# Where a two-layer graph network fetches its last results, turns its raw features and checks its adjacency

## The chip, the cores and the metric

The kernel runs on one core of one Trainium2 chip. TensorE (PE) multiplies matrices, with its weight loads shown as PEld; VectorE is DVE, ScalarE is ACT, GpSimd is POOL and SyncE is SP. SP and POOL also issue most of the DMA transfers, each in the order of its own queue. The metric is the time of one execution on the device in microseconds (us); the median of three executions is compared.

## The reference, cut to what matters

Sixteen graphs of 1024 nodes with 128 features go through two layers. Each normalizes its input, runs four rounds over the graph's 1024 x 1024 adjacency of zeros and ones, and adds the result to its input.

```python
# layer 0: a gated network, per graph
h = relu(layernorm(x))
for i in range(4):
    hw = einsum('bnc,cd->bnd', h, weight[i])
    m = einsum('bjn,bjd->bnd', adj, hw)
    h = gru_cell(m, h, w_ih[i], w_hh[i], b_ih[i], b_hh[i])
x = x + h * mask[:, :, None]
# layer 1: four convolutions; mean and variance go over all graphs and nodes
h = relu(layernorm(x))
for i in range(4):
    h = relu(einsum('bnm,bmc->bnc', adj, h @ W[i]) + b[i])
    mu, var = mean(h, (0, 1)), mean(square(h - mu), (0, 1))
    h = gamma[i] * (h - mu) * rsqrt(var + EPS) + beta[i]
x = x + h
```

## The kernel before, in words

**The gated stage.** Two streams run side by side: `sa` takes the even graphs and `sb` the odd ones, one layer apart by half a step. `half_step(one, two)` does the gates of `two` (`products`, twelve pairs of matmuls in two halves of 512 nodes, then sigmoid, tanh and the DVE arithmetic that ends in `mixed`) and the aggregation of `one` over the adjacency (`agg_step`, L523). `clock[0]` counts the half steps, from 3. In this stage every engine gets its instructions in the order of the program text (`tc.manual_schedule`). Extra work is put into an agenda by `at(n, place, go)` and taken out by `due(place)` at named places of half step n: "beside0" and "beside1" lie after the reset gate of each half, "looks" just after "beside0" and ahead of the first tanh, "gap" after the second half is done and ahead of the aggregation, "start" at the beginning. An instruction in the agenda thus stands in each engine's order at that place, whatever the other engines have reached.

`row_sums` (L602) lets ACT sum rows of the first graph's adjacency; its scratch tile `junk` has the same single buffer as the transposed weights `w_both`, which a matmul (`join_layer`, L488) reads. The sums leave as `degree`, which the convolutions use. `glance` and `look` collect in `low` whether any adjacency value is inexact in bfloat16. After the gated stage the maximum of `low` becomes `worst` (a DVE reduction and a minimum), a one-column matmul adds it over the partitions (`pt_flag`, L1337), and DVE copies it to `flag_i` (L1338), which chooses another path at the very end. These instructions stand outside the hand-written order, so a scheduler places them.

At the end of a graph's four rounds `half_away` transposes the last h in 32 x 32 blocks on DVE and stores it, half by half, to a DRAM tile `pair`, from which it is read back in another order (`pair_in`, L620). For the last two graphs, 14 and 15, the store goes through POOL, and the tail of the layer is done as `chores` during the first convolution: fetch of the pair into the tile `feat[b]`, masked sums and statistics (`masked_sum` L729, `norm_sums` L662 and L663), `factors` (root, reciprocal, and the store of the new x to `xmid_d`, L743), `blocks` (normalization and relu on ACT, L678, written over x), and the store of the result to `ymid_d` (L746).

**The first convolution.** A loop goes over batches b, one graph each. `load_adjT` lets SP load eight row tiles (256 KB each) of the transposed adjacency in bfloat16: even batches into the single tile `block`, odd ones into the ring `half` of eight buffers (`packed`). DVE and ACT cast them to `wide` (a ring of twelve). `first_split` loads y of the next batch through POOL (L1426), after a one-column POOL copy that waits until the tile's earlier reader is done (L1425); ACT rounds it to `hw[0]` (L1429), DVE writes the remainder to `hw[1]` (L1430). `aggregate` does 32 matmuls per batch in two halves. Between the halves PE does `first_weights` of the batch before: ACT copies two banks to `cm` (L1439), PE multiplies (L1440), ACT applies relu into `feat` (L1408) and DVE takes statistics (L1417). In this stage a scheduler fixes each engine's order ahead of time from the program and its own estimates; it may place chores earlier than the text has them, but each engine then runs strictly in that order.

`raw_turned(1)` transposes feat of graph 0 on DVE (L1449), stores it and loads it back through POOL (L1452, L1456), for `raw_split(1)` at the last batch.

Of the kernel before, what the change touches and what calls it, by code (L numbers as in the profile page):

```python
# [8 lines left out]
F32 = mybir.dt.float32  # L9
F32R = mybir.dt.float32r  # L10
BF16 = mybir.dt.bfloat16
# [3 lines left out]
ALU = mybir.AluOpType  # L15
AX = mybir.AxisListType
P = 128
HALF = 512
# [323 lines left out]
def exact_path(  # L342
# [21 lines left out]
    nc = tc.nc  # L364
# [17 lines left out]
    def tmp(name):  # L382
        return ps_t.tile([P, HALF], F32, tag="tmp", name=name)
# [148 lines left out]
    with ExitStack() as st:  # L532
# [83 lines left out]
        def pair_in(d, t, eng=nc.sync):  # L616

            src = d.rearrange("h (t r) (s x) -> s r (h t) x", t=4, s=4)
            for s in range(4):
                eng.dma_start(t[s * 32 : (s + 1) * 32, :].rearrange("r (a x) -> r a x", a=8), src[s])  # L620
# [96 lines left out]
        def half_out(t, src, hf, name, d=None, eng=nc.sync):  # L717
            turned = nc.vector.transpose(by_nodes(t), four_ways(src[:, hf * HALF : (hf + 1) * HALF]))
            return exchange_out(t, f"{name}_{hf}", d, eng), turned

        def cross_tile(name):
            return half_tile(name).bitcast(F32)
# [22 lines left out]
        def store_ymid(b, y):  # L745
            nc.gpsimd.dma_start(ymid_d[b], y)  # L746
# [3 lines left out]
        class Stream:  # L750
# [15 lines left out]
            def sums(self, ks):  # L766
                norm_sums(self.xt, self.norm, ks)
# [93 lines left out]
            def fetch(self):  # L861

                if self.i == 3 and self.b + 2 < B and not written[0]:
                    if self is sa:
                        t = turned_tile(f"stage{self.b + 2}").bitcast(F32)
                        room[0] = [t[:, 2 * q : 2 * q + 2, :].rearrange("p a n -> p (a n)") for q in range(4)]
                    self.stage = room[0]
                    stage_rows(self.b + 2, self.stage, range(2))
# [36 lines left out]
            def half_away(self, hf):  # L905

                if self.i + 1 - hf == L:
                    end = self.b + 2 >= B
                    if hf == 0 and end:
                        self.pair = dram.tile([NH, P, HALF], F32, tag=f"end{self.b}", name=f"pair_end{self.b}")  # L910
                    elif hf == 0:
                        self.pair = rawd.tile([NH, P, HALF], F32, tag="pair", name=f"pair_out{self.b}", bufs=4)
                    eng = nc.gpsimd if end else nc.sync
                    half_out(cross_tile(f"t_out{self.b}_{hf}"), self.new, hf, f"out{self.b}", self.pair[hf], eng)
                elif self.turned_away(self.i + 1 - hf):
                    nm = f"{self.b}_{self.i + 1 - hf}"
                    out, self.last_dve = half_out(cross_tile(f"t_h{nm}_{hf}"), self.new, hf, f"h{nm}")
                    self.outs.append(out)
# [154 lines left out]
        def at(n, place, go):  # L1073
            agenda.setdefault((n, place), []).append(go)
# [9 lines left out]
        def half_step(one, two, gated=None, halfway=None, rest=None):  # L1084

            due("ins")
            due("start")
            if one.i > 0:
                one.halves_back()
            else:  # L1090
                one.hw = hw_tiles(one.b, f"ghw{one.b}_0")
            two.fetch()
            due("load")
            two.products(0)
            two.reset_gate(0)
            due("beside0")
            due("looks")
            two.fetch_more()
            two.candidate(0)
            two.less(0)  # L1100
            two.update_gate(0)
            two.scaled()
            one.high(0)
            one.low(0)
            two.mixed(0)
            two.half_away(0)
            two.first_four()
            if (clock[0], "mid") in agenda or (clock[0], "words") in agenda:
                paced(two.new[:, :1], f"mid{clock[0]}")
                due("words")  # L1110
                due("mid")
            two.products(1)
            two.reset_gate(1)
            one.high(1)
            due("beside1")
            two.first_glances()
            one.low(1)
            two.candidate(1)
            two.less(1)
            two.update_gate(1)  # L1120
            two.last_four()
            two.scaled()
            two.mixed(1)
            two.half_away(1)
            due("outs")
            if gated:
                gated()
            due("gap")
            if (clock[0], "behind") in agenda:
                paced(two.new[:, N - 1 :], f"gap{clock[0]}")  # L1130
                due("behind")
            due("end")
            one.agg_step(0)
            if halfway:
                halfway()
            one.agg_step(1)
            if rest:
                rest()
            two.finish()
            clock[0] += 1  # L1140
# [4 lines left out]
        with tc.manual_schedule(engines=every):  # L1145
# [149 lines left out]
            def ahead(i):  # L1295
                join_layer(i)
                if i == 2:
                    turn_hh(3)
# [1 line left out]
            sa.plan(0)  # L1300
            sb.plan(1)
            for n, place, js in (
                (5, "beside1", (0,)),
                (6, "beside0", (1,)),
                (6, "beside1", (2,)),
                (6, "gap", (3,)),
                (7, "gap", (4, 5, 6)),
                (8, "start", (7,)),
            ):
                at(n, place, lambda js=js: row_sums(sa.rows, js))  # L1310

            def degree_out():
                d = degree_d.rearrange("(s j i o) -> s i o j", s=4, j=4, i=32)
                for k in range(4):
                    nc.gpsimd.dma_start(d[k], by_row[k * 32 : (k + 1) * 32, :].rearrange("i (o j) -> i o j", o=2))

            at(9, "mid", degree_out)
            half_step(sa, sb, looks, lambda: ahead(1))
            half_step(sb, sa, lambda: both(2), lambda: ahead(2), lambda: turn_ih(prep, w_g, 3))
            written[0] = False  # L1320
# [8 lines left out]
                sb.gate_step(hf)  # L1329
                sb.half_away(hf)  # L1330


    worst = small.tile([P, 1], F32, tag="worst", name="worst")
    nc.vector.tensor_reduce(worst, low, axis=AX.X, op=ALU.max)
    nc.vector.tensor_scalar_min(worst, worst, 1.0)
    pt = tmp("pt_flag")
    nc.tensor.matmul(pt[:1, :1], worst, ones, start=True, stop=True)  # L1337
    nc.vector.tensor_copy(flag_i, pt[:1, :1])  # L1338


    feat_pool = ctx.enter_context(tc.tile_pool(name="feat", bufs=1))
# [3 lines left out]
    def load_adjT(b, i):  # L1345
        ts = []
        block = None if b % 2 else turned_tile(f"block{b}_{i}")
        for j in range(NB):
            t = half_tile(f"packed{b}_{i}_{j}") if b % 2 else block[:, j, :]
            nc.sync.dma_start(t, adjT_d[b][j])  # L1350
            r = row_tile(f"wide{b}_{i}_{j}")
            if j % 3 == 1:
                nc.scalar.copy(r, t)  # L1353
            else:
                nc.vector.tensor_copy(r, t)  # L1355
            ts.append(r)
        return ts
# [155 lines left out]
    def chores(s, b):  # L1513

        xt, parts = s.xt, feat[b]
        y = xt.rearrange("p k c -> p (k c)")
        nt = norm_tiles(f"mid{b}")

        def sums(q):
            ks = range(2 * q, 2 * q + 2)  # L1520
            masked_sum(b, xt, parts, ks)
            norm_sums(xt, nt, ks)

        def factors():
            norm_factors(nt)
            store_xmid(b, xt)

        def blocks(hf):
            norm_blocks(xt, y, nt, range(hf * BH, (hf + 1) * BH))

        return [
            (0, lambda: pair_in(s.pair, parts, nc.gpsimd)),
            *((1 + q, lambda q=q: sums(q)) for q in range(4)),
            (4, factors),
            (5, lambda: blocks(0)),
            (6, lambda: blocks(1)),
            (6, lambda: store_ymid(b, y)),
        ]

    late = {}  # L1540
    for s, b, first in ((sa, B - 2, 1), (sb, B - 1, 5)):
        for k, go in chores(s, b):
            late.setdefault(first + k, []).append(go)

# [2 lines left out]
    stats = small.tile([P, B * NH + 1, 6], F32, tag="bn_st", name="stats0")  # L1547
    hw, waiting, hw_last = first_split(0), None, None
    for b in range(B):
        rows = load_adjT(b, 0)  # L1550
        hw_next = first_split(b + 1, hw_last) if b + 1 < B else None
        pm = banks(b, 0)
        aggregate(pm, hw, rows, 0)
        if waiting:
            first_weights(*waiting, stats)
        for go in late.get(b, ()):
            go()
        if b == B - 1:
            hw_next = raw_split(1)
        aggregate(pm, hw, rows, 1)  # L1560
        if b == 4:
            raw_turned(1)
        if b == 2:
            nc.gpsimd.dma_start(degree, degree_d.partition_broadcast(P))
        hw_last, hw, waiting = hw, hw_next, (b, pm)
# [117 lines left out]
```

## Time and profile before

| quantity | value |
|---|---|
| median of three executions | 1773.37 us (1772.59 to 1776.34) |
| the profiled execution | 1774.41 us |
| its span, first to last instruction | 1772.4 us |
| mean granted TensorE clock | 0.996 |
| gated stage | up to 1145.46 us of the span |
| first convolution, batch 0 to batch 6 | 1145.46 to 1210.45 us |
| one half step undisturbed (114.41 to 131.98) | 17.57 us |
| one batch of the first convolution undisturbed | 9.03 us |

The profile shows one execution. For each group of instructions it gives the busy time, the mean time of one, and the idle time of the engine just before, with what ended it. Idle time of PE costs time, since PE is nearly always busy; idle time of another engine costs only where PE waits for it later. A timeline gives start, duration, instruction and, in brackets, the idle time before it and its releaser. All times within the run are microseconds from the span's start.

### The profile page before, as it was taken

How to read it: one execution, taken by the hardware profiler on the slowest of the kernel's cores; microseconds unless marked ns; L12 is line 12 of the kernel's file. 1: busy time of each engine (PE TensorE's matmuls, PEld its weight loads, DVE VectorE, ACT ScalarE, POOL GpSimd, SP SyncE). 2: the span in 40 equal slices, each digit the busy share in tenths (PEclk: the TensorE clock that was granted, in tenths of full speed). 3: DMA queues.
4: the chain of work that ended last, by engine and by line, in shares of the span. 5: the costliest groups of instructions: out<-in, count | busy, mean ns of one | idle time of the engine just before them, and what ended most of it. 6: DMA issues, size and time to landing. Idle time of an engine off the chain costs nothing. (4 is left out here: it accounts for less than half of the span.)

```text
span 1772.4 us, 22193 instructions
## 1 busy us (share of the span) xinstructions
PE 1745.7 (98%) x6654; PEld 1184.6 (67%) x6654; DVE 1321.6 (75%) x2378; ACT 1145.5 (65%) x1821; POOL 398.2 (22%) x452
## 2 busy tenths in 40 slices
PE   9999999999999999999999999998999999999997
PEld 5665656565656565665656555666778888888886
DVE  7777987887787887887888787675666666666665
ACT  6467556656556657565655654467787768768865
POOL 4314323232341331331422423231000001000010
PEclk9999999999999999999999999999999999999999
DMA  8449468368557656746846826899867667757666
GB/s 287 128 117 269 123 178 280 111 172 257 159 161 212 199 154 193 234 132 179 256 126 173 285 87 183 264 306 369 279 217 243 227 248 232 262 201 264 216 232 257
DMA packets 305313, 375.50 MB, mean 212 GB/s; under 512 B 24876, under 2 KB 189520, under 8 KB 305184
## 3 DMA queue, kind: packets, MB, share of 16 engines
q1 hardware_dynamic: 292864, 334.06, 60.5%
q0 software_dynamic: 11792, 39.68, 6.5%
q8 instruction: 54, 0.88, 0.2%
q14 instruction: 75, 0.61, 0.1%
q10 hardware_dynamic: 528, 0.26, 0.0%
HBM read 272.19 MB, written 101.72 MB: 211 GB/s over the span
## 5 line engine op out<-in xcount | busy, mean ns | idle before, releaser
L523 PE MATMUL pm<-row,ghw 128*128 128x512 f32 x2048 | 504.4, 403 | 0.8 <-POOL row L562 0.4
L523 PEld LDWEIGHTS pm<-row,ghw 128*128 128x128 f32 x2048 | 383.8, 188 | 108.1 <-issue 22.5
L523 PE MATMUL pc_m<-wide,chw 128*128 128x512 f32 x1024 | 245.3, 395 | 0.0
L523 PEld LDWEIGHTS pc_m<-wide,chw 128*128 128x128 f32 x1024 | 190.6, 188 | 42.5 <-issue 4.3
L968 ACT COPY m<-pm 128x512 f32<-128x512 f32 x128 | 68.7, 588 | 219.2 <-PE pm L523 219.2
L587 POOL CAST row<-stage 128x1024 fp32r<-128x1024 f32 x112 | 126.8, 1137 | 343.9 <-DMA stage<-in_adj_dram 260.2
L523 PE MATMUL pc_g_r<-wide,chw 128*128 128x512 f32 x464 | 188.3, 406 | 0.4 <-DVE wide L1355 0.4
L523 PE MATMUL pc_g_z<-wide,chw 128*128 128x512 f32 x464 | 181.4, 391 | 0.0
L1030 ACT ACTIVATE r<-r,vecs 128x512 f32<-128x512 f32 x128 | 92.2, 720 | 127.0 <-DVE r L1027 124.9
L633 POOL CAST pair<-row 128x1024 bf16<-128x1024 f32 x128 | 165.8, 1345 | 32.8 <-DVE adjT L639 32.8
L1026 DVE SCALAR_TENSOR_TENSOR r<-g_hn,vecs,r 128x512 f32<-128x512 f32 x128 | 93.2, 728 | 105.0 <-ACT r L1025 54.0
L1355 DVE CAST wide<-packed 128x1024 fp32r<-128x1024 bf16 x160 | 109.3, 690 | 72.8 <-PE pc_g_z L523 50.0
L1355 DVE CAST wide<-block 128x1024 fp32r<-128x1024 bf16 x160 | 109.8, 692 | 67.8 <-PE pc_m L523 40.5
L1353 ACT CAST wide<-packed 128x1024 fp32r<-128x1024 bf16 x96 | 100.9, 1052 | 53.4 <-PE pc_g_z L523 21.1
L1007 PE MATMUL g_r<-m,w_mT 128*128 128x512 f32 x256 | 130.8, 592 | 0.4 <-ACT m L968 0.4
L1007 PE MATMUL g_xn<-m,w_mT 128*128 128x512 f32 x256 | 130.7, 592 | 0.0
L1007 PE MATMUL g_z<-m,w_mT 128*128 128x512 f32 x256 | 130.7, 592 | 0.0
L1353 ACT CAST wide<-block 128x1024 fp32r<-128x1024 bf16 x96 | 100.6, 1049 | 45.0 <-PE pc_g_z L523 20.1
L1025 ACT ACTIVATE r<-g_r,brz 128x512 f32<-128x512 f32 x128 | 87.9, 687 | 57.0 <-PE g_r L1007 56.6
L1417 DVE BATCH_NORM_STATS2 stats<-feat 128x6 f32<-128x512 f32 x129 | 85.3, 683 | 43.0 <-ACT feat L1408 29.8
L1043 DVE TENSOR_TENSOR h<-h,r 128x512 f32<-128x512 f32 x96 | 69.8, 727 | 51.9 <-ACT r L1030 51.5
L1047 DVE TENSOR_TENSOR h<-h,z 128x512 f32<-128x512 f32 x128 | 95.0, 742 | 16.3 <-ACT z L1034 3.6
(200 smaller groups left out, 2908.5 us busy)
## 6 DMA issues: line engine op xcount, KB each, us to landing
block<-adjT_d SPq DMA_DIRECT2D x256, 256.0 KB, 4.7
packed<-adjT_d SPq DMA_DIRECT2D x256, 256.0 KB, 5.5
stage<-in_adj_dram SPq DMA_DIRECT2D x120, 512.0 KB, 5.6
adjT_d<-adjT SPq DMA_DIRECT2D x64, 512.0 KB, 7.3
cross_h<-t_h SPq DMA_DIRECT2D x94, 256.0 KB, 2.1
n_h<-cross_h SPq DMA_DIRECT2D x376, 64.0 KB, 2.1
xmid_d<-x POOLq DMA_DIRECT2D x16, 512.0 KB, 3.8
x<-in_x_dram SPq DMA_DIRECT2D x15, 512.0 KB, 4.4
```

The costliest lines, as they stand in the source:

```text
L523: nc.tensor.matmul(pm[hf], hw[s][:, j * P : (j + 1) * P], rows[j][:, hf * HALF : (hf + 1) * HALF], start=(j == 0 and s == 0), stop=(j == N ...
L587: nc.gpsimd.tensor_copy(t, stage[j % 4])
L633: nc.gpsimd.tensor_copy(halves[:, :, o], rows[4 * o + j].bitcast(F32))
L1007: nc.tensor.matmul(po, wT[:, i, g * C : (g + 1) * C], rhs, start=start, stop=stop)
L1025: nc.scalar.activation(r, pr, AF.Sigmoid, bias=brz[:, 3 * i : 3 * i + 1])
L1026: nc.vector.scalar_tensor_tensor(r, phn, b_hn(i), r, ALU.add, ALU.mult)
L1030: nc.scalar.activation(self.r, self.r, AF.Tanh, bias=b_in(self.i))
L1043: nc.vector.tensor_sub(ho, hin, self.r)
L1047: nc.vector.tensor_mul(ho, ho, self.z)
L1353: nc.scalar.copy(r, t)
L1355: nc.vector.tensor_copy(r, t)
L1417: nc.vector.bn_stats(stats[:, b * NH + hf + k, :], dst)
```

## The change

Five things move; no arithmetic is taken out or added.

- The fetch of the last h (graphs 14 and 15) gets a POOL copy ahead of it that reads the current batch's `hw[1]`, so it waits for that DVE remainder. Chores begin one batch later in the text (2 and 6 instead of 1 and 5), and `blocks` a further batch later.
- The transposed halves of the last h go to a tile of the `pair` ring instead of two tiles of the `half` ring. DVE's casts of batch 1 are ordered behind the last DVE instruction of the gated stage; in the resulting order of SP, the loads of batch 1 stand ahead of those of batch 2.
- `raw_turned(1)` moves from batch 4 to batch 12, the thirteenth.
- The row sum of row 0 moves from "beside1" to "gap" in half step 5, that of row 4 from "gap" to "looks" in half step 7.
- The flag's reduction, minimum and matmul go into the hand-written order, in the gap of half step 60 (B * L - 2 * L + 4), and the copy to `flag_i` into the gap of half step 61. Before, the scheduler had them in half steps 58 and 59.

```diff
+                    if end and hf == 0:
+                        t = work.tile([P, 2 * N], BF16, tag="pair", name=f"t_end{self.b}", bufs=3).bitcast(F32)
+                        self.ends = [t[:, k * HALF : (k + 1) * HALF] for k in range(NH)]
+                    t = self.ends[hf] if end else cross_tile(f"t_out{self.b}_{hf}")
+                    half_out(t, self.new, hf, f"out{self.b}", self.pair[hf], eng)
...
-                (5, "beside1", (0,)),
+                (5, "gap", (0,)),
...
-                (7, "gap", (4, 5, 6)),
+                (7, "looks", (4,)),
+                (7, "gap", (5, 6)),
...
+            def worst_of_all():
+                worst = small.tile([P, 1], F32, tag="worst", name="worst")
+                nc.vector.tensor_reduce(worst, low, axis=AX.X, op=ALU.max)
+                nc.vector.tensor_scalar_min(worst, worst, 1.0)
+                pt = tmp("pt_flag")
+                nc.tensor.matmul(pt[:1, :1], worst, ones, start=True, stop=True)
+                at(end + 5, "gap", lambda: nc.vector.tensor_copy(flag_i, pt[:1, :1]))
+
+            end = B * L - 2 * L
+            at(end + 4, "gap", worst_of_all)
...
+        def fetch(seen):
+            nc.gpsimd.tensor_copy(parts[:, :1], seen[:, :1].bitcast(F32))
+            pair_in(s.pair, parts, nc.gpsimd)
...
-            (5, lambda: blocks(0)),
-            (6, lambda: blocks(1)),
-            (6, lambda: store_ymid(b, y)),
+            (6, lambda seen: blocks(0)),
+            (7, lambda seen: blocks(1)),
+            (7, lambda seen: store_ymid(b, y)),
...
-    for s, b, first in ((sa, B - 2, 1), (sb, B - 1, 5)):
+    for s, b, first in ((sa, B - 2, 2), (sb, B - 1, 6)):
...
+        if b == 1:
+            with tc.issue_after(sb.last_dve.ins):
+                rows = load_adjT(b, 0)
...
-            go()
+            go(hw[1])
...
-        if b == 4:
+        if b == 12:
             raw_turned(1)
```

More of the change, by code (lines that the diff above doesn't have):

```diff
@@ L913, in half_away @@
                     eng = nc.gpsimd if end else nc.sync
-                    half_out(cross_tile(f"t_out{self.b}_{hf}"), self.new, hf, f"out{self.b}", self.pair[hf], eng)
+                    if end and hf == 0:
[3 more added lines that the diff above has]
+                    half_out(t, self.new, hf, f"out{self.b}", self.pair[hf], eng)
                 elif self.turned_away(self.i + 1 - hf):
@@ L1330, in exact_path @@
                 sb.half_away(hf)
[L1333 to L1338, printed above, removed]
     feat_pool = ctx.enter_context(tc.tile_pool(name="feat", bufs=1))
@@ L1529, in blocks @@
             norm_blocks(xt, y, nt, range(hf * BH, (hf + 1) * BH))
+        def fetch(seen):
+            nc.gpsimd.tensor_copy(parts[:, :1], seen[:, :1].bitcast(F32))
+            pair_in(s.pair, parts, nc.gpsimd)
         return [
-            (0, lambda: pair_in(s.pair, parts, nc.gpsimd)),
-            *((1 + q, lambda q=q: sums(q)) for q in range(4)),
-            (4, factors),
-            (5, lambda: blocks(0)),
-            (6, lambda: blocks(1)),
-            (6, lambda: store_ymid(b, y)),
+            (0, fetch),
+            *((1 + q, lambda seen, q=q: sums(q)) for q in range(4)),
+            (4, lambda seen: factors()),
+            (6, lambda seen: blocks(0)),
+            (7, lambda seen: blocks(1)),
+            (7, lambda seen: store_ymid(b, y)),
         ]
     late = {}
-    for s, b, first in ((sa, B - 2, 1), (sb, B - 1, 5)):
+    for s, b, first in ((sa, B - 2, 2), (sb, B - 1, 6)):
         for k, go in chores(s, b):
@@ L1549, in exact_path @@
     for b in range(B):
-        rows = load_adjT(b, 0)
+        if b == 1:
+            with tc.issue_after(sb.last_dve.ins):
+                rows = load_adjT(b, 0)
+        else:
+            rows = load_adjT(b, 0)
         hw_next = first_split(b + 1, hw_last) if b + 1 < B else None
```

## The prediction

> **What bounds the kernel now.** I read the busy times first, then TensorE's waits, then the timelines of the engines around each wait.
>
> ```profile
> PE 1745.7 (98%) x6654; PEld 1184.6 (67%) x6654; DVE 1321.6 (75%) x2378; ACT 1145.5 (65%) x1821; POOL 398.2 (22%) x452
> ```
>
> TensorE (PE) is busy 98% of the 1772.4 us, and no edit here takes matrix work away: both kernels issue the same matmuls. So the change is worth what it does to PE's few idle stretches, and what new ones it makes. In the list of who waited for whom (total, times, longest), one wait dominates:
>
> ```profile
> PE pw_g_hn L1440 <- ACT cm L1439: 8.1, 3, 5.8
> ```
>
> It lies in the first convolution. PE's timeline (start, duration, instruction, idle before it) places the three:
>
> ```profile
> 1176.61 1.12 PE L1440 MATMUL pw_g_hn<-cm,w_c 128*128 128x512 f32 x2 [0.89 <-ACT cm L1439]
> 1187.37 1.12 PE L1440 MATMUL pw_g_hn<-cm,w_c 128*128 128x512 f32 x2 [1.49 <-ACT cm L1439]
> 1202.42 2.07 PE L1440 MATMUL pw_g_hn<-cm,w_c 128*128 128x512 f32 x2 [5.76 <-ACT cm L1439]
> 1204.28 1.92 PE L1440 MATMUL pw_g_xn<-cm,w_c 128*128 128x512 f32 x2
> ```
>
> After the 5.76 us the pairs of matmuls take 2 us instead of 1.02. The table by stretch (busy time of PE, weight loads, DVE, ACT, POOL, then granted clock, DMA share, GB/s) says why:
>
> ```profile
> 1192.90:1210.50 17.60, 11.84 (x38) 7.92 (x37) 8.53 (x17) 11.01 (x21) 1.84 (x4) 0.81 1.02 385
> 1210.50:1219.50 9.00, 9.00 (x38) 6.74 (x37) 5.71 (x8) 8.55 (x16) 2.87 (x5) 1.00 1.04 391
> ```
>
> The granted clock is 0.81 in the batch of the long wait and 1.00 in the next: a pause costs its length and then a slow stretch. ACT's and POOL's timelines show what held ACT's copy `cm`:
>
> ```profile
> 1197.97 1.65 ACT L678 ACTIVATE x<-x,ms_mid,rs_mid 128x128 f32<-128x128 f32 x4 [5.00 <-DMA xmid_d<-x]
> 1201.79 1.05 ACT L1439 COPY cm<-pc_m 128x512 f32<-128x512 f32 x2
> ```
> ```profile
> 1189.27 1.36 POOL L743 DMA_DIRECT2D xmid_d<-x  x1
> ```
>
> ACT stood before a normalization (`blocks`) that overwrites x, until the store of x had landed; POOL had issued that store only at 1189.27, behind four raw-feature loads, and it took 8.6 us among queued loads. `cm` is behind `blocks` in ACT's order.
>
> Two other places matter. At the flag (half step 59; 60 and 61 follow):
>
> ```profile
> 1039.31 0.19 PE L1337 MATMUL pt_flag<-ones,worst 128*1 128x1 f32 x2
> 1040.49 7.36 PE L523 MATMUL pm<-row,ghw 128*128 128x512 f32 x30 [0.33 <-DVE ghw L945]
> 1057.59 7.84 PE L523 MATMUL pm<-row,ghw 128*128 128x512 f32 x32
> 1063.21 0.71 DVE L718 STREAM_TRANSPOSE t_h<-h 128x512 f32<-128x512 f32 x1
> 1075.17 7.84 PE L523 MATMUL pm<-row,ghw 128*128 128x512 f32 x32
> 1079.39 0.71 DVE L718 STREAM_TRANSPOSE t_h<-h 128x512 f32<-128x512 f32 x1
> ```
>
> PE starts each aggregation (L523) about 5 us before DVE transposes the second half of the step. And early, in the row sums:
>
> ```profile
> 92.17 1.06 ACT L602 ACTIVATE junk<-row 128x1024 bf16<-128x1024 f32 x1 [6.62 <-PE pt_wm L488]
> 103.16 1.13 PE L1007 MATMUL g_hn<-h,w_hhT 128*128 128x512 f32 x2 [0.56 <-DVE r L1026]
> 133.41 1.12 PE L1007 MATMUL g_r<-m,w_mT 128*128 128x512 f32 x2 [0.40 <-ACT m L968]
> ```
>
> **Row sums: -1.9 us.** The first sum stood ahead of a tanh and waited 6.62 us for a matmul that reads its scratch tile. Behind the tanh it waits with only a weight copy and the m copies behind it (m is due at 95.5, the matmul is over at 92.1), so nothing is late. The step that began at 95.57 ended at 114.41, 18.84 us against 17.57 for the next: -1.27. Later, sums 4 to 6 hold the m copy: the step from 131.98 reached its aggregation in 10.57 us against 9.90: -0.67. Sum 4 moves into ACT's 1.86 us of idleness before the tanh at 120.85; one sum is 1.06 + 0.19. Bounds: -1.94 and 0.
>
> **The flag, old place: -1.2 us.** Step 59 runs from 1028.92 to 1047.69, 18.77 against 17.57: DVE's copy of the flag waited 3.86 us for PE and stood ahead of `low(0)`.
>
> **The flag, new place: +8.1 us.** In step 60 DVE's reduction now stands behind the second transpose, and PE's one-column matmul waits for it, ahead of the aggregation in PE's order. So everything on PE queues behind DVE. Transpose end minus aggregation start was 6.33 us in step 60 (1063.92 - 1057.59), 4.93 in step 61, 4.06 in step 63 (1114.37 - 1110.31). Step 60 was late because the old flag copy delayed DVE a step earlier; I take 4.93. Add the reduction 0.29, the minimum 0.14, and about 0.2 for the matmul: 5.5 us (4.7 to 7.0). After it a slow stretch: none followed the pause of 1.49 us, one followed 5.76. That one cost 1210.45 - 1202.42 = 8.03 against 5.39 for the same instructions from 1214.09, so 2.6. PE would idle some 5.0 us, nearer to 5.76: I take 2.6 and keep 0 as the other end. In all 8.1, from 4.7 to 9.6. The copy of the flag comes a step later and waits for nothing.
>
> [...]
>
> **The first convolution, removed: -12.2 us.** Batch 1 began on PE at 1153.13 and batch 6 at 1210.45: 57.3 us for five batches that take 9.03 each undisturbed (1210.45 to 1219.48), 45.15. This holds the three waits, 0.41 for a late row tile, and the slow stretch. The raw features (two transposes, two stores, four loads on POOL's queue) leave this place; at batch 12 they stand on POOL ahead of one y load, which is due some 18 us later, and cost nothing; without that cover it would be the 5.5 us that a raw store takes. Loads of batch 1 now precede those of batch 2 on SP's queue, so the 0.41 goes.
>
> **The first convolution, added: +3.4 us.** Call batch 0's start on PE zero; batch k then starts at 7.7 + 9.05(k-1), and its middle, where `cm` of batch k-1 is due, is 3.6 later. The fetch of sample 14 now waits, through a POOL copy, for batch 2's DVE remainder. Behind that copy on POOL stand four fetch DMAs and all y loads. Ahead of it, POOL's first pace copy now waits for the last transposed h to be stored: its issue at about 1150.0, 4.22 to land, so 8.9. The y load of batch 2 follows at 9.6 and needs 4.4 to 5.5: 14 to 15, ACT's split 1, DVE's 1.2, due at 17.2: it fits by a little. Then the pace copy and four fetches, 17.0 to 19.4. In the trace fetches took 5.2 to 7.5 us, so they land near 24.5; batch 4's y load, 7.3 as at 1163.93, near 26.7, and `cm` of batch 2 makes its 29.4. DVE then does in its order eight masked sums (0.25 each), five casts (0.6), a remainder (1.15) and statistics (3.1 in all) up to the last masked sum: 9.2 us, 33.7. The store of x goes out there. It needs 3.84 us in quiet stretches and 8.6 to 9.6 in this one; with one y load and eight row loads beside it I take 5.5, so 39.3. In ACT's new order the first `blocks` stands behind that store, and ahead of batch 5's split and `cm` of batch 3: 0.45 + 0.95 + 0.55 gives 41.2, due at 38.45: a wait of 2.8. No slow stretch (2.8 is nearer to 1.49). Restarts and small misses 0.6. With the short landing 1.6 in all, without any wait 0; with the long one 6.5 and a slow stretch, and late fetches on top, 12.2 as before.
>
> Sample 15 has the same order, but its last masked sum ends 0.7 us into batch 7 and its `cm` is due 12 us later, so it costs nothing unless the store takes over 7 us.
>
> **Sum.** -1.9 - 1.2 + 8.1 - 12.2 + 3.4 = -3.8 us. The profiled execution took 1774.41 us (span 1772.4): 1770.6. It lies 1.04 over the median of 1773.37, so for the median 1769.6.
>
> **Rivals.**
> - The old wait stays (0.2). Speaks for it: ACT still stands before `blocks` for a store that was 8.6 to 9.6 us under way here. Against: the raw transfers are gone from beside it. The addition is then 9 to 12.2 instead of 3.4: 1775.2 to 1778.4. It makes the kernel slower than the median at an addition over 7.2, by over 0.2% (3.5 us; about what a measurement tells from no change) over 10.7.
> - The first convolution runs clean, 0 to 1.6 added (0.2): 1766.2 to 1767.8. For it: the waits spread the transfers. Against: `blocks` has no distance to its store in ACT's order.
> - The flag costs little (0.1): if DVE ends earlier and no slow stretch follows, 4.7 or less: 1766.2 or below. Against: the transpose is 4 us late in every step looked at.
> - The waits don't spread the work (0.1): DVE's sums are as dense as before, and splits of batches 2 to 4 come late by 1 to 2 us each: 1771 to 1774, no change.
>
> My forecast has 0.4, with 1768 to 1773 as its own range; 0.17 of it lie more than 3.5 us under the median. Faster: these, the clean case and the cheap flag, 0.47. Same: the rest of the forecast, the fourth rival's upper part and a little of the first, 0.33. Slower: 0.2. Range 1764 to 1777.5, which leaves out the worst of the first rival and both gains together.
>
> **What would show it.** Right: PE's wait list names the flag matmul with DVE's `worst` and 4 to 6 us; `pw_g_hn` for `cm` falls under 4 us; the waits at 103 and 133 vanish; ACT's idle time before `blocks` names the store. Wrong: the clock falls in neither or both places, or a batch's split waits for its y load.

## The result, and the profile after

The changed kernel takes 1779.44 us (median of 7, 1776.05 to 1780.74), the kernel before 1773.45 us beside it (median of 7, 1772.45 to 1776.34). The ratio is 1.003, 95% interval 1.0018 to 1.0042: slower by 3 to 7 us, where 3.8 us faster was forecast. The profiled execution is the median one, 1779.44 us, with a span of 1777.5.

The busy times of the page say as before that PE decides:

```profile
PE 1747.2 (98%) x6654; PEld 1187.1 (67%) x6654; DVE 1320.9 (74%) x2378; ACT 1146.4 (64%) x1821; POOL 399.8 (22%) x454
```

The list of waits of PE in the changed kernel (total, times, longest) has the same sum for `cm` as before, 8.1 us, and two new rows:

```profile
PE pw_g_hn L1448 <- ACT cm L1447: 8.1, 2, 5.3
PE pt_flag L1327 <- DVE worst L1325: 4.3, 1, 4.3
PE g_r L1011 <- DMA h_in<-pair_in: 1.4, 1, 1.4
```

PE's timeline of the changed kernel (start, duration, instruction, idle time before it and its releaser) places them:

```profile
184.95 1.10 PE L1011 MATMUL g_r<-h_in,w_hhT 128*128 128x512 f32 x2 [1.38 <-DMA h_in<-pair_in]
...
1046.16 1.02 PE L1011 MATMUL g_r<-h,w_hhT 128*128 128x512 f32 x2
...
1060.88 0.19 PE L1327 MATMUL pt_flag<-ones,worst 128*1 128x1 f32 x2 [4.26 <-DVE worst L1325]
1061.00 9.08 PE L523 MATMUL pm<-row,ghw 128*128 128x512 f32 x32
1069.92 1.02 PE L1011 MATMUL g_r<-h,w_hhT 128*128 128x512 f32 x2
...
1182.41 1.12 PE L1448 MATMUL pw_g_hn<-cm,w_c 128*128 128x512 f32 x2 [2.80 <-ACT cm L1447]
...
1198.63 2.07 PE L1448 MATMUL pw_g_hn<-cm,w_c 128*128 128x512 f32 x2 [5.33 <-ACT cm L1447]
```

The half step with the flag runs from 1046.16 to 1069.92, 23.76 us against 17.57: +6.19. DVE's timeline shows what the flag's matmul stood behind:

```profile
1059.74 0.71 DVE L718 STREAM_TRANSPOSE t_h<-h 128x512 f32<-128x512 f32 x1
1060.38 0.26 DVE L1324 TENSOR_REDUCE worst<-low 128x1 f32<-128x144 f32 x1
1060.67 0.15 DVE L1325 TENSOR_SCALAR worst<-worst 128x1 f32<-128x1 f32 x1
```

The first convolution has two waits for `cm` where it had three. ACT's timeline of the changed kernel shows what each `cm` stood behind:

```profile
1180.83 1.05 ACT L1437 CAST chw<-feat 128x1024 fp32r<-128x1024 f32 x1 [5.58 <-DMA feat<-ymid_d]
1181.78 1.07 ACT L1447 COPY cm<-pc_m 128x512 f32<-128x512 f32 x2
...
1196.67 0.49 ACT L678 ACTIVATE x<-x,ms_mid,rs_mid 128x128 f32<-128x128 f32 x1 [6.18 <-DMA xmid_d<-x]
1197.07 1.03 ACT L1437 CAST chw<-feat 128x1024 fp32r<-128x1024 f32 x1
1198.00 0.57 ACT L1447 COPY cm<-pc_g_r 128x512 f32<-128x512 f32 x1
```

The first stands behind the split of batch 4, which waits for its y load; the second behind the normalization that overwrites x, which waits for x's store, as before the change. POOL's timeline gives the issues:

```profile
1167.64 2.51 POOL L620 DMA_DIRECT2D feat<-pair_end  x4 [0.24 <-POOL feat L1433]
...
1188.32 0.92 POOL L743 DMA_DIRECT2D xmid_d<-x  x1 [0.83 <-DVE st_mid L662]
```

By the records of the transfers, the four fetches landed between 1173.0 and 1178.8. The y load issued behind them at 1170.14 landed at 1180.73, 10.6 us later, and the store of 1188.32 at 1196.58, 8.26 us later, beside one y load and eight row loads issued between 1186.72 and 1190.82, and four more row loads before it had landed.

Two stages hold the whole difference. The table gives the start of the first convolution on PE (what the gated stage cost), and the time from the first `pw_g_hn` of batch 1's middle to that of batch 6's: five batches, 45.15 us undisturbed (5 x 9.03). From there to PE's last matmul every kernel of this study but one needs the same 546.8 to 547.0 us; the one is named below. Both columns are of one profiled execution each. Seven of these kernels have the gated stage of the kernel before, and in them the convolution starts between 1145.03 and 1145.94; so a difference below about 1 us in that column says little by itself.

| kernel | median, us | before beside it | ratio (95%) | convolution starts | five batches |
|---|---|---|---|---|---|
| before | 1773.45 | | | 1145.46 | 57.33 |
| changed | 1779.44 | 1773.45 | 1.003 (1.0018 to 1.0042) | 1150.11 | 58.01 |
| flag alone | 1778.70 | 1772.60 | 1.0032 (1.0020 to 1.0044) | 1150.93 | 54.39 |
| row sums alone | 1771.84 | 1772.60 | 0.9991 (0.9982 to 1.0000) | 1143.97 | 56.79 |
| row sums, degrees later | 1770.70 | 1772.60 | 0.9989 (0.9980 to 0.9998) | 1143.46 | 55.85 |
| convolution's edits alone | 1773.38 | 1772.60 | 1.0004 (0.9995 to 1.0013) | 1145.94 | 57.21 |
| raw features alone | 1771.67 | 1772.51 | 0.9994 (0.9985 to 1.0003) | 1145.70 | 54.23 |
| before, not in place | 1770.32 | 1773.01 | 0.9982 (0.9973 to 0.9991) | 1145.03 | 51.86 |
| convolution's edits, not in place | 1767.81 | 1773.01 | 0.9964 (0.9952 to 0.9977) | 1145.24 | 50.35 |
| the same, fetch behind the y load | 1766.67 | 1773.01 | 0.9958 (0.9944 to 0.9971) | 1145.59 | 51.68 |
| convolution's edits, begun later | 1763.65 | 1773.07 | 0.9949 (0.9936 to 0.9963) | 1145.07 | 45.13 |
| flag, matmul a half step later | 1772.69 | 1773.01 | 0.9991 (0.9982 to 1.0000) | 1144.32 | 57.13 |
| all mended | 1759.27 | 1772.51 | 0.9931 (0.9918 to 0.9945) | 1142.75 | 45.21 |
| all mended, early fetch | 1764.72 | 1772.51 | 0.9957 (0.9943 to 0.9970) | 1142.98 | 51.47 |

The changed kernel's profiled execution lost 4.65 us in the gated stage and 0.68 in the first convolution.

### The profile page after: what moved, and what is told of

Read it like the earlier page. It is cut to its first block, busy times and chain, and to the rows that moved or that the text cites. A ratio compares the mean times of both kernels' runs of the same rounds, so it can differ in the third digit from the quotient of the medians.

```text
span 1777.5 us, 22209 instructions
## 1 busy us (share of the span) xinstructions
PE 1747.2 (98%) x6654; PEld 1187.1 (67%) x6654; DVE 1320.9 (74%) x2378; ACT 1146.4 (64%) x1821; POOL 399.8 (22%) x454
## 5 line engine op out<-in xcount | busy, mean ns | idle before, releaser
L523 PEld LDWEIGHTS pc_m<-wide,chw 128*128 128x128 f32 x1024 | 191.4, 189 | 43.2 <-issue 4.9
L1425 DVE BATCH_NORM_STATS2 stats<-feat 128x6 f32<-128x512 f32 x129 | 85.3, 683 | 43.2 <-ACT feat L1416 30.0
```

Source lines behind the costliest of these rows:

```text
L523: nc.tensor.matmul(pm[hf], hw[s][:, j * P : (j + 1) * P], rows[j][:, hf * HALF : (hf + 1) * HALF], start=(j == 0 and s == 0), stop=(j == N ...
L1425: nc.vector.bn_stats(stats[:, b * NH + hf + k, :], dst)
```

## The experiments

Lines of code are those of the profile of each kernel, so they shift by a few with its edits. The expectations call a graph a sample.

### One part of the change at a time

**The flag alone.** Reduction, minimum, matmul and copy as the change has them, in an otherwise unchanged kernel.

> The kernel before with the flag alone moved. Theory: the one-column matmul waits 4 to 5 us for DVE's reduction ahead of an aggregation, the clock halves for one window of 3.4 us, and half step 59 loses its late copy: +6.2 - 1.2 = +5.0 us. By the prediction's two terms it is +6.9. Rival: the loss of the changed kernel lies in its first convolution, and the flag costs 0 to 1 us.

PE's timeline of this kernel:

```profile
1061.08 0.19 PE L1322 MATMUL pt_flag<-ones,worst 128*1 128x1 f32 x2 [4.26 <-DVE worst L1320]
```

The same 4.26 us, and the gated stage ends 5.48 us later. The half step is 6.81 us longer than 17.57 here; from 1055 to 1070 the mean granted clock is 0.77, where the changed kernel had 0.89. The median is 6.1 us higher than that of the kernel before beside it. So the flag by itself costs as much as the whole change lost; the rival falls.

**The row sums alone.**

```diff
-                (5, "beside1", (0,)),
+                (5, "gap", (0,)),
...
-                (7, "gap", (4, 5, 6)),
+                (7, "looks", (4,)),
+                (7, "gap", (5, 6)),
```

> The kernel before with the row sums alone moved. Theory: the two late steps shrink by 1.9 us until 135 us, but PE then waits about 1.4 us near 185 us for the loads of h_in, whose landing is not set by PE: -0.5 us in all. Rival: that wait in the changed kernel was a chance of one execution, and -1.9 stays.

The waits at 103 and 133 us are gone: the two late steps take 17.57 and 17.58 us here, 1.27 and 0.70 less than before. In all fourteen kernels the step from about 95 us takes 18.82 to 18.85 us with the sums in their old place and 17.57 with them in the new one. No wait for `h_in` came: its last load landed at 181.54, while it landed at 184.82 in the changed kernel and at 184.57 before. So the wait of 1.4 us doesn't come with every execution of the moved sums, as the rival has it, and the run with the convolution's edits alone, with the sums in the old place, has one of 0.35 us. The gated stage ended 1.49 us earlier and not 1.97, mainly because a later step (from 1080.45) took 0.79 us longer; why, was not found. The median fell by 0.8 us, with no change inside the interval, so it doesn't tell the theory from the rival.

**The row sums, and the degrees stored later.**

```diff
-            at(9, "mid", degree_out)
+            at(13, "mid", degree_out)
```

> The kernel before with the row sums moved, and the four stores of the degrees moved from half step 9 to half step 13. Theory: these stores of scattered elements hold the queues from 166 to 181 us and set when h_in lands; without them there the wait near 185 us is gone and -1.9 us stays, unless the stores make another load late at half step 13 (then a wait of 1 to 4 us near 240 us). Rival: the loads of raw adjacency set the landing, and the wait of 1.4 us stays: -0.5 us.

`h_in` landed at 176.18, over 5 us earlier, and the gated stage ended 2.00 us earlier than before; no step near half step 13 became longer. These stores do set when `h_in` lands: issued at 164 to 168 us, they landed 11 to 14 us later in the kernel before, in the changed kernel and with the row sums alone, and the last loads of `h_in`, issued behind them, landed after them. Before the change PE needed `h_in` at 185.40 and had 0.83 us to spare; a gain of 1.9 us ahead of it was more than that. The edit takes away a risk rather than a steady cost; its median lies 1.9 us under that of the kernel before.

**The convolution's edits alone** (spread chores, raw features at the thirteenth batch; flag and row sums as before).

> The kernel before with the edits of the first convolution alone (spread fetches and sums, the turned raw features at the thirteenth batch). Theory: two new waits, some 2.8 us for the split of batch 4 behind its late y load and some 5.3 us for the normalization behind its store, take the place of the three old ones, each with a slow stretch: 0 to +0.5 us. The prediction's terms give -8.8. Rival: these waits come from the 4.7 us by which the gated stage ended later, and alone the edits gain 4 us or more.

PE's timeline:

```profile
1177.56 1.13 PE L1442 MATMUL pw_g_hn<-cm,w_c 128*128 128x512 f32 x2 [1.92 <-ACT cm L1441]
...
1193.55 2.07 PE L1442 MATMUL pw_g_hn<-cm,w_c 128*128 128x512 f32 x2 [5.09 <-ACT cm L1441]
```

The two waits of the changed kernel are there with the gated stage unchanged, and the median moves by +0.8 us, with an interval of -0.9 to +2.3: nothing is gained. The prediction's two terms for this stage, -8.8 together, fall, and so does the rival.

**The raw features alone.**

```diff
-        if b == 4:
+        if b == 12:
             raw_turned(1)
```

> The kernel before with the raw features turned at the thirteenth batch instead of the fifth, and nothing else. Theory: the store of x of sample 14 no longer stands behind four raw loads, leaves some 2 us earlier and lands beside less traffic, so the long wait of 5.8 us shrinks but stays, since the overwriting still awaits the landing: -1 to -4 us. Rival: the raw transfers were what made that landing 8.6 us, and the wait is gone: -8 us, as the prediction's removal would have it.

PE's and POOL's timelines:

```profile
1191.04 2.08 PE L1440 MATMUL pw_g_hn<-cm,w_c 128*128 128x512 f32 x2 [5.17 <-ACT cm L1439]
```
```profile
1181.16 0.91 POOL L743 DMA_DIRECT2D xmid_d<-x  x1 [0.15 <-DVE st_mid L662]
```

The store now leaves at 1181.16 instead of 1189.27, with no raw transfer beside it, and still lands only 7.8 us later (1188.99). The two short waits of the kernel before (0.89 and 1.49 us) are gone in this execution, and a wait for a row tile grew from 0.41 to 1.30 us; since the other kernels with an unchanged convolution have short waits for `cm` of 0.30 to 1.64 us, and one or two of them, that may be chance. The long one stays: 5.17 us, against 5.76 to 6.93 in those five. The rival falls. Whether this part gains at all is open: 0.9994 with 1 inside the interval, and 54.23 us for the five batches lies just under the spread of the unchanged convolution (54.39 to 57.33 in the five kernels that don't touch it).

### What holds `cm`

**Before, but not in place.** One line: the normalization writes to the feature tile, which the masked sums have read by then.

```diff
         xt, parts = s.xt, feat[b]
-        y = xt.rearrange("p k c -> p (k c)")
+        y = parts
```

> The kernel before, with one edit: the normalization of the last two samples writes to the sample's feature tile, which the masked sums have read, instead of overwriting x. Theory: what holds PE in the first convolution is that overwriting, which must await the landing of x's store; without it the 5.8 us wait and its slow stretch of 2.6 us are gone with no spreading at all: -8.4 us; the waits of 0.9 and 1.5 us stay. Rival: the transfers as a whole are too dense here, and the split behind late y loads waits next in its place: 0 to -4 us.

ACT's timeline at the same place:

```profile
1185.54 0.49 ACT L678 ACTIVATE feat<-x,ms_mid,rs_mid 128x128 f32<-128x128 f32 x1 [1.35 <-DVE ms_mid L674]
1185.94 1.03 ACT L1429 CAST chw<-feat 128x1024 fp32r<-128x1024 f32 x1
1186.87 0.58 ACT L1439 COPY cm<-pc_g_r 128x512 f32<-128x512 f32 x1
```

The 5 us behind the store are gone, though the store still took 8.9 us to land; what is left before the normalization is 1.35 us for DVE's factors, and PE waits 1.79 us there. The five batches take 51.86 us, 2.5 to 5.5 less than in the kernels whose convolution is otherwise the same; the median falls by 2.7, not by 8.4. The cause of the long wait is shown, the size was too large: shorter waits remain, 0.92 us for a row tile and 0.65, 1.79 and 0.69 for `cm`, the 1.79 with a slow stretch (granted clock 0.50 from 1187.71 to 1191.12).

**The convolution's edits, and not in place.** The same line on top of the convolution's edits.

> The first convolution's edits alone, and the normalization written to the feature tile instead of over x. Theory: of the two new waits the second (5.1 us, near 1193) and its slow stretch of 2.6 us vanish, the first (1.9 us and its slow stretch, behind the late y load) stays: -6.9 us against the kernel before. Rival: the late y load of the next batch takes the place of the store, and the gain is under 4 us.

The second wait is gone and from the middle of batch 4 on a batch takes 9.03 us. PE's timeline keeps the first:

```profile
1178.03 1.79 PE L1442 MATMUL pw_g_hn<-cm,w_c 128*128 128x512 f32 x2 [2.85 <-ACT cm L1441]
```

The five batches go from 57.21 to 50.35 us, 6.9 less, as the theory has it; the median lies 5.2 us under that of the kernel before (interval 4.1 to 8.5).

**The same, with the fetch behind the y load.** `early[b]` is called right after `first_split` of the following batch.

```diff
+            if k == 0:
+                early[first + 1] = go
+            else:
                 late.setdefault(first + k, []).append(go)
...
         hw_next = first_split(b + 1, hw_last) if b + 1 < B else None
+        if b in early:
+            early[b](hw_last[1])
```

> As the run before it, and the four fetches of the last h issued behind the y load of the next batch but one on POOL's queue instead of ahead of it. Theory: that load then lands some 3 us earlier, the split of batch 4 is in time, and the wait of 1.9 us with its slow stretch of 1.7 us vanishes too: -10.5 us against the kernel before. Rival: the eight row loads on SP's queue set that landing, not the order of POOL's: no change against the run before it.

The y load of batch 4, issued at 1163.12, landed at 1171.21, and the split was in time. But one batch later ACT's timeline has this:

```profile
1187.01 0.30 ACT L666 ACTIVATE rs_mid<-mv_mid,eps_t 128x8 f32<-128x8 f32 x1 [3.29 <-DVE mv_mid L663]
1187.21 1.03 ACT L1431 CAST chw<-feat 128x1024 fp32r<-128x1024 f32 x1
1188.15 0.57 ACT L1441 COPY cm<-pc_g_r 128x512 f32<-128x512 f32 x1
```

The square root stands ahead of split and `cm` in ACT's order and waits for DVE's last statistics; PE waits 4.02 us at 1188.78. The theory was right on the load and wrong on the sum: the wait moved on. The interval overlaps that of the run before it, so nothing more is shown to be gained.

**The convolution's edits, begun later, still in place.**

```diff
-    for s, b, first in ((sa, B - 2, 2), (sb, B - 1, 6)):
+    for s, b, first in ((sa, B - 2, 4), (sb, B - 1, 6)):
```

> The first convolution's edits alone, with one number changed: sample 14's fetch and sums begin at the fifth batch instead of the third; the normalization still overwrites x in place. Theory 1: overwriting in place behind the store is enough for a wait wherever it stands, so about 5 us with a slow stretch remain some two batches later, and the gain against the kernel before is 4 us at most. Theory 2: it takes the traffic of batches 2 to 5 as well, where row loads catch up and the store lands after 8 us instead of 4 to 6.6; later there is room, as for sample 15: no wait in the first convolution, -11 us.

The five batches take 45.13 us: no wait is left for graph 14. Its store still took 7.0 us to land (1192.31 to 1199.29), but ACT came to the normalization only 0.5 us too early, and no `cm` was late. One wait came further on, in batch 8, for graph 15. The timelines of ACT and PE:

```profile
1199.37 0.49 ACT L678 ACTIVATE x<-x,ms_mid,rs_mid 128x128 f32<-128x128 f32 x1 [0.50 <-DMA xmid_d<-x]
...
1213.80 0.30 ACT L666 ACTIVATE rs_mid<-mv_mid,eps_t 128x8 f32<-128x8 f32 x1 [2.50 <-DVE mv_mid L663]
1217.65 0.49 ACT L678 ACTIVATE x<-x,ms_mid,rs_mid 128x128 f32<-128x128 f32 x1 [2.03 <-DMA xmid_d<-x]
```

```profile
1222.67 1.13 PE L1442 MATMUL pw_g_hn<-cm,w_c 128*128 128x512 f32 x2 [2.97 <-ACT cm L1441]
```

There the root was late by 2.50 us and the normalization by 2.03 us for its store (7.0 us to land). This is the kernel whose rest is longer, 550.1 us. So theory 1 falls and theory 2 is nearer, with the size off by one wait: 9.4 us gained at the median. Its reason holds in part only: the store took 7.0 us and not 4 to 6.6. The room was in ACT's order, which reached the normalization 6.6 us behind the issue of the store.

### Mending the parts

**The flag, its matmul a half step later.**

```diff
+                at(end + 5, "gap", lambda: flag_sum(worst))
+
+            def flag_sum(worst):
                 pt = tmp("pt_flag")
                 nc.tensor.matmul(pt[:1, :1], worst, ones, start=True, stop=True)
-                at(end + 5, "gap", lambda: nc.vector.tensor_copy(flag_i, pt[:1, :1]))
+                at(end + 6, "gap", lambda: nc.vector.tensor_copy(flag_i, pt[:1, :1]))
```

> The kernel before with the flag moved as in the change, but the one-column matmul a whole half step behind its reduction. Theory: only its place ahead of the aggregation in the same gap cost time, so the wait of 4.3 us and the slow window vanish, and the late copy in half step 59 is gone as well: -1.2 us. Rival: DVE's reduction behind the second transpose delays the step by itself: +1 us or more.

PE's timeline:

```profile
1074.17 0.19 PE L1325 MATMUL pt_flag<-ones,worst 128*1 128x1 f32 x2
```

No wait for `worst`: the half step with the reduction takes 17.58 us. The half step of the flag's old place takes 17.57 instead of 18.77, and that of the matmul's new place 17.92, 0.35 more than undisturbed; the gated stage ends 1.14 us earlier than before. The rival falls, and the loss of the flag was the place of one matmul.

**All mended.** The changed kernel with: normalization to the feature tile, and y of the last two graphs left there instead of stored and loaded again; graph 14 begun at the fifth batch; the flag's matmul later; degrees at half step 13.

> The changed kernel with four edits: the normalization written to the feature tile (and so no store and load of y for the last two samples), sample 14's fetch and sums begun at the fifth batch instead of the third, the flag's matmul a half step behind its reduction, the degrees stored at half step 13. Theory: no wait is left in the first convolution, as its fifth and later batches had none: -1.6 for the row sums, -0.9 for the flag, -12.2 for the convolution, together -14 us against the kernel before. Rival: the sums of both samples beside each other, or the fetches in the fifth batch, make a new wait of 2 to 4 us: -8 to -11 us.

The head of PE's wait list:

```profile
PE pt_idle L1156 <- POOL ident masks.py:199: 2.4, 1, 2.4
PE pt_wm L488 <- ACT w_both L482: 0.7, 1, 0.7
PE g_z L1011 <- ACT z L1038: 0.6, 1, 0.6
```

Neither `cm` nor the flag is in it. The first convolution takes its 45.2 us, the gated stage 2.71 us less than before. 1759.27 us: 13.2 us under the kernel before, by its interval 9.7 to 14.5, as the theory has it. That is about 19 us under the changed kernel, each taken against the kernel before beside it. Four edits stand in it together; that y of the last two graphs stays in its tile was not tried alone.

**All mended, with the early fetch.** As the run before it, but graph 14 fetched in the third batch behind the y load, and the root one batch later in the text.

> As the run before it, but sample 14 is still fetched in the third batch, behind the y load, with its square root one batch later. Theory: the fetches fall among the row loads of the first batches, which come late of themselves, and DVE's in-order sums hold ACT and so PE for 2 to 4 us in one place: -9 to -12 us. Rival: with the square root later nothing waits: -14 us, as the run before it.

ACT's timeline:

```profile
1184.34 0.30 ACT L666 ACTIVATE rs_mid<-mv_mid,eps_t 128x8 f32<-128x8 f32 x1 [3.31 <-DVE mv_mid L663]
```

PE waits 3.43 us in batch 4's middle; ACT's root again waits 3.31 us for DVE's statistics ahead of split and `cm`. The scheduler placed the root at the same spot in spite of the text, so the rival was not tried. The theory's wait came; the gain of 7.8 us (interval 5.3 to 10.1) lies just under its 9 to 12. What helps is the later place; why the sums are in time there, these runs don't tell.

## Why the prediction was wrong

- **What bounds the kernel**: right. The difference of the two kernels is made of PE's waits and their slow stretches.
- **Row sums, -1.9**: right in mechanism and size: the two late steps lost 1.97 us where the sums alone were moved and 1.77 in the changed kernel. What it left out is what is late next: `h_in`, with 0.83 us to spare, made two later steps of the changed kernel's profiled execution 1.65 us longer. The run with the sums alone had no such wait, so this part is chance.
- **Flag, old place, -1.2**: right; the half step takes 17.57 us instead of 18.77 wherever the flag was moved.
- **Flag, new place, +8.1**: right in mechanism, mis-sized: +6.2. The aggregation started 4.94 us late (5.5 forecast), since the transpose ended 4.39 us behind the start that was due (4.93 taken), and the slow stretch cost 1.25 (2.6 forecast): from its start to the next step 8.92 us instead of 7.67. With the flag alone, at the lower mean clock from 1055 to 1070 (0.77 against 0.89), it cost 1.87 (9.54 us).
- **First convolution, removed, -12.2**: one execution's figure. In five kernels with this convolution unchanged the five batches took 54.39 to 57.33 us, so the loss is 9.2 to 12.2.
- **First convolution, added, +3.4: the step that failed.** It measured 12.9 in the changed kernel and 12.1 alone. The 12.9 are the waits of 2.80 and 5.33 us and 4.7 for slow stretches and small misses; forecast were one wait of 2.8, no slow stretch, and 0.6. From batch 0's start the times were: fetches landed at 22.9 to 28.7 (near 24.5 forecast), batch 4's y load at 30.6 (26.7), the store of x issued at 38.2 (33.7), landed at 46.5 (39.3), `cm` of batch 3 done at 48.5 (41.2); by then it was due at 43.2 (38.45), as PE itself was late. Two terms of it failed. The y load was taken as 7.3 us and as hidden; behind four fetches it took 10.6 and cost a wait of 2.8. The landing of the store was taken as 5.5, between 3.84 in quiet stretches and 8.6 in this one; it took 8.26, and 7.8 even with no raw transfer near. The row of the same store in the same stretch was the nearest, and it was put aside for a reason, the raw transfers, that their removal alone disproves: with y and row loads alone beside it the store was no quicker than 7.8.
- **"No slow stretch"** after a wait of 2.8 us: wrong; the granted clock was 0.50 from 1183.66 to 1187.07.
- **Sample 15 costs nothing**: right. Its store took 6.6 us and no `cm` was late.
- **The rivals**: the first, "the old wait stays", is what happened, with the price it named (addition 9 to 12.2) just passed. The argument against it was the raw transfers again. A late split, of which the fourth rival speaks, came beside it.
- **What would show it**: of the signs of being right all came but one, `cm` under 4 us (it was 5.3). Both signs of being wrong came: the granted clock fell in both places (to 0.50 from 1060.77 to 1064.19, and from 1183.66 to 1187.07), and the split of batch 4 waited for its y load.

In the profiled executions the terms make -1.77 for the row sums, +1.65 for `h_in`, -1.20 and +6.19 for the flag and +0.68 for the first convolution (forecast -8.8). With 0.21 us by which the step from 95 us began earlier that is +5.34; the two stages gave 4.65 + 0.68 = 5.33. The first convolution was thus 9.5 us too low in the forecast, and by luck the flag, 1.9 too high, hid a part of it.

## What to carry to other kernels

An instruction placed on the bounding engine should stand at least one step behind the one that feeds it on another engine: one matmul of 0.19 us in the same gap cost 6.2 us here, a step later 0.35. A write in place waited for the store that reads the old value, and what stood behind it in its engine's order waited too (5.00 us before, 6.18 in the changed kernel): write to a tile that is free, or put as many microseconds of other work between them as the store takes in that stretch. Price a transfer from the row of the same transfer in the same stretch, and run the one edit that is to shorten it before counting on that.

## What was not expected of the hardware

The length of a pause did not tell whether a slow stretch followed. The prediction expected one behind the long pauses and none behind 2.8 us; the profiled executions show this (idle time of PE, and the granted clock in or behind it):

| pause, us | kernel | measured |
|---|---|---|
| 0.89 and 1.49 | before | clock 1.00 from 1171.90 to 1192.90 |
| 1.79 | before, not in place | 0.50 from 1187.71 to 1191.12 |
| 2.80 | changed | 0.50 from 1183.66 to 1187.07 |
| 2.97 | begun later | the rest took 3.1 to 3.3 us more than in the other kernels, 0.1 to 0.3 beside the pause |
| 4.02 | fetch behind | 0.50 from 1189.89 to 1193.30 |
| 4.26 | changed | 0.50 from 1060.77 to 1064.19 |
| 5.33 | changed | 0.50 from 1197.31 to 1204.14 |
| 5.76 | before | 0.51 from 1200.80 to 1207.70 |

The table by stretch (length, then busy time of PE, weight loads, DVE, ACT, POOL, then granted clock, DMA share, GB/s) shows the stretch with the pause of 1.79 us and the one behind it in "before, not in place", then the three slow stretches of the changed kernel:

```profile
1184.30:1187.71 3.41, 1.62 (x8) 1.04 (x7) 3.41 (x13) 2.17 (x4) 1.72 (x4) 1.00 0.65 206
1187.71:1191.12 3.41, 3.41 (x5) 1.33 (x5) 3.41 (x10) 3.41 (x7) 3.02 (x4) 0.50 0.86 272
```
```profile
1060.77:1064.19 3.42, 3.31 (x10) 2.60 (x11) 3.42 (x5) 0.00 (x0) 2.15 (x2) 0.50 0.85 297
1183.66:1187.07 3.41, 3.41 (x8) 2.13 (x7) 3.41 (x9) 2.95 (x4) 0.93 (x2) 0.50 0.69 253
1197.31:1204.14 6.83, 5.51 (x9) 3.06 (x10) 3.12 (x4) 6.83 (x13) 1.12 (x2) 0.50 0.96 347
```

So a pause of 1.79 us was followed by half clock in one execution, and one of 2.97 us cost little beyond its own length in another. In the changed kernel half clock lasted about 3.4 us twice and 6.83 us once. What decides this, these runs don't show.

The unchanged first convolution varied by 2.9 us between the profiled executions of five kernels, as much as several of the edits were worth; for such edits the stage times of one execution say where the time went, and only the medians say whether anything was gained.
